# A graph-attention layer: look_rows moved behind the weights, lookups without an addition, low parts in two wide operations, counts cleared on ScalarE

## The chip, the cores and the metric

The kernel runs on one core of a Trainium2 chip. A core has a matrix engine (PE), a vector engine (DVE), a scalar engine (ACT), a general engine that here only issues gathers (POOL), and a queue engine for other transfers (SP). The metric is the device time of one execution in microseconds; the kernel before is given by the median of three executions.

## The reference

There are 12500 nodes with 64 features, 400000 edges with 64 features each, a source node `src` drawn evenly and a target node `dst`; the edges are sorted by target, and low targets have far more edges than high ones. All numbers are float32.

```
e     = leaky_relu(concat(x[src], x[dst], edge) @ W_attn + b_attn, 0.01)[:, 0]
m     = concat(x[src], edge) @ W_ne
alpha = softmax of e over the edges of each target
z     = segment_sum(alpha[:, None] * m, dst)
out   = layernorm(x + relu(concat(x, z) @ W_out))
```

## The kernel before

**Groups, lots, batches.** The edges are cut into 782 groups of 512 (128 partitions by T = 4). 678 of them go the ordinary way, in 44 batches, mostly of 16 groups in four lots of four. For each group and t POOL issues one indirect gather (L310) of 128 rows of a table, which holds a node's share of the score and its features; the rows land in `zx`, of which there are eight buffers, two batches' worth. A lot's scores come from its edge rows `ze` (L344, L346), the gathered column (L351), and the target's share through a one-hot `hot` (L353 to L362). Then a batch goes through one segment softmax (L652 to L714): scans along the 128 columns of a line on DVE, and turns of boundary values between partitions and lines by PE (L556, L559) with copies by ACT (L659, L563). The softmax is a generator with four stops; at each of them `dense_step(n)` puts other work between. After it the weights w are made (L749), and PE multiplies them with `zx` (L763): this frees the buffers of `zx` for POOL's next gathers. The products of the first two lots are issued in the same batch, those of the others during the next one; DVE adds their sums at L780 (`add_up`).

**Dense groups.** The first 104 groups have few target nodes each. Their sources are not gathered. In some 35 batches three of them are done beside the ordinary work:

- *Lookups.* `look_row` loads the low parts of the group's source numbers, spread over all partitions, into `low_of`; `look_turn` makes a one-hot of them on ACT (L400, L401); `look_products` multiplies it with the nodes' shares on PE (L411); `look_scores` picks by the high part on DVE (L436 to L440) and adds to `y_dense` (L442). `look_rows` makes the edges' and targets' shares of all three groups (L421 to L428) and writes their sum to `y_dense` (L430).
- *Sums.* When a round of dense groups has been through its softmax, `dense_counts` counts, for one group, the weights by low and high part of the source: ACT makes one-hots of the high parts (L450, L451), DVE the weighted one-hots of the low parts, `lows` (L453), PE multiplies them (L458), and `dense_sum` adds the result to `counts` (L475). After each chunk `node_products` (L525) multiplies counts with the nodes' features, `node_pick` takes what is wanted (L533, L536) and clears `counts` (L538). `edge_products` and `edge_sum` (L510, L518) do the edge part.

**Order.** The program orders PE, DVE, ACT and SP by hand: every engine works in the order of the program. POOL's gathers are issued a batch ahead and wait only for buffers. Inside a batch: at lot 0 the loads of `ed` and `wrow_d` (`look_loads`) and of the first `low_of`; scores of lot 0, `node_products`, `edge_products`; after the scores of lot 1 `add_up`, the second one-hot, the products of the first lookup, and `dense_counts` of the first group; after the scores of lot 2 `look_rows`; scores of lot 3; the softmax with its steps; the weights and the products of lots 0 and 1; `slots_of`, which prepares the batch after next. In step 0 of the softmax stand `node_pick`, `edge_sum`, the first `look_scores` and `dense_sum`; in step 1 the second `look_scores`; in steps 2 and 3 `dense_counts` of the second and third group. `ed`, `wrow_d` and `low_of` have one buffer each.

Of the kernel before, what the change touches and what calls it, by code (L numbers as in the profile page):

```python
# [9 lines left out]
F32 = mybir.dt.float32  # L10
I32 = mybir.dt.int32
AF = mybir.ActivationFunctionType
OP = mybir.AluOpType
AX = mybir.AxisListType

P = 128
T = 4
# [8 lines left out]
S = 48  # L26
BG = 32
BIG = 6
LOWS = 6
SG = 4  # L30
BS = 16
DO = BS + 1
# [10 lines left out]
ND = 16  # L43
# [11 lines left out]
EngineType = mybir.EngineType  # L55


def sorted_path(ctx, tc, x, dst, idx, edge, w_ne, w_attn, b_attn, w_out, out, flag):
# [6 lines left out]
    nc = tc.nc  # L65
    N, D = x.shape
    E = edge.shape[0]
    NB = (N + P - 1) // P
# [6 lines left out]
    within = "a destination is a node"  # L75

    const = ctx.enter_context(tc.tile_pool(name="const", bufs=1))
# [32 lines left out]
    def nodes_of(g):  # L110
        return next(n for upto, n in NODS if g < upto)
# [4 lines left out]
    def round_of(g):  # L116
        return max(d for d in range(DB) if begins[d] <= g)

    def kept_at(g):
        d = round_of(g)  # L120
        return g - begins[d] + d % 2 * BD
# [3 lines left out]
    DN = DBL * P  # L125
# [47 lines left out]
    low, place = (const.tile([P, T, DG], F32, name=n) for n in ("low", "place"))  # L173
    high, slot_ = (const.tile([P, T, DG], BF16, name=n) for n in ("high", "slot_"))
    y_dense = const.tile([P, T, 2 * BD], F32, name="y_dense")
    kept = const.tile([P, T, 2 * BD], F32, name="kept")
# [4 lines left out]
    acce = const.tile([P, DN + NOD], F32, name="acce")  # L181
    nc.vector.memset(acce, 0.0)
    edge_both = const.tile([P, D], F32, name="edge_both")
    dn = const.tile([1, DG + 1], I32, name="dn")
    rel = const.tile([1, DG], I32, name="rel")
    counts = const.tile([P, NB, ND], F32, name="counts")
# [3 lines left out]
    nc.vector.tensor_reduce(node, ident.rearrange("p (h n) -> p n h", n=ND), axis=AX.X, op=OP.add)  # L190
    meet = const.tile([1, 2], I32, name="meet")
    of_next = const.tile([1, 4], F32, name="of_next")
    scrap_row = const.tile([1, 1], F32, name="scrap_row")

    loop = ExitStack()
# [2 lines left out]
    tiny = loop.enter_context(tc.tile_pool(name="tiny", bufs=2))  # L198
# [28 lines left out]
    pens, sixth, count_ = cut(pps, 2 * P, P, P)  # L227
    sixth, w_dst = sixth[:, 0:NB], sixth[:, 0:D]
# [164 lines left out]
    def big():  # L393
        return work.tile([P, P, T], F32, name="big", bufs=BIG)
# [19 lines left out]
    def look_rows(g0, n, loads):  # L414

        ed, wrow = loads
        many = nodes_of(g0)
        assert many == nodes_of(g0 + n - 1)
        pr = feats.tile([P, SG, T, D], F32, name="pr", bufs=1)
        total = tiny.tile([P, 2, EACH, T], F32, name="total")[:, :, 0:n]  # L420
        nc.vector.tensor_tensor(pr[:, 0:n], ed[:, 0:n], w_edge.unsqueeze(1).to_broadcast([P, n, T, D]), op=OP.mult)  # L421
        nc.vector.tensor_reduce(total[:, 0], pr[:, 0:n], axis=AX.X, op=OP.add)
        at = pr[:, 0].rearrange("p t f -> p (t f)")[:, 0:n * T * many].rearrange("p (g t n) -> p g t n", g=n, n=many)
        nc.vector.tensor_tensor(at, slots[:, 0:many].unsqueeze(1).unsqueeze(1).to_broadcast([P, n, T, many]),
                                slot_[:, :, g0:g0 + n].rearrange("p t g -> p g t").unsqueeze(3).to_broadcast([P, n, T, many]),
                                op=OP.is_equal)
        nc.vector.tensor_tensor(at, at, wrow[:, 0:n].unsqueeze(2).to_broadcast([P, n, T, many]), op=OP.mult)
        nc.vector.tensor_reduce(total[:, 1], at, axis=AX.X, op=OP.add)  # L428
        y0 = kept_at(g0)
        nc.vector.tensor_tensor(y_dense[:, :, y0:y0 + n].rearrange("p t g -> p g t"), total[:, 0], total[:, 1], op=OP.add)  # L430

    def look_scores(g, found):

        pr = feats.tile([P, SG, T, D], F32, name="pr", bufs=1)
        hits = pr.rearrange("p g t f -> p (g t f)")[:, 0:T * NB].rearrange("p (t h) -> p t h", t=T)
        nc.vector.tensor_tensor(hits, count_[:, 0:NB].unsqueeze(1).to_broadcast([P, T, NB]),  # L436
                                high[:, :, g:g + 1].to_broadcast([P, T, NB]), op=OP.is_equal)
        nc.vector.tensor_tensor(hits, hits, found, op=OP.mult)  # L438
        picked = tiny.tile([P, T], F32, name="picked")
        nc.vector.tensor_reduce(picked, hits, axis=AX.X, op=OP.add)  # L440
        y = y_dense[:, :, kept_at(g)]
        nc.vector.tensor_tensor(y, y, picked, op=OP.add)  # L442

    def dense_counts(g):

        highs, lows = [], []
        wide = NB * min(FIT, nodes_of(g))
        for t in range(T):
            hi = big().rearrange("l p t -> l (p t)")[:, 0:wide]
            nc.scalar.activation(hi, places[:, 0:wide], AF.Square, bias=place[:, t, g:g + 1])  # L450
            nc.scalar.activation(hi, hi, AF.Relu, scale=-1.0, bias=1.0)  # L451
            lows.append(work.tile([P, P], F32, name="lows", bufs=LOWS))
            nc.vector.tensor_scalar(lows[t], count_, low[:, t, g:g + 1], kept[:, t, kept_at(g):kept_at(g) + 1],  # L453
                                    op0=OP.is_equal, op1=OP.mult)
            highs.append(hi)
        to = psum.tile([P, SG, P], F32, name="pg", bufs=4).rearrange("p a b -> p (a b)")[:, 0:wide]
        for t in range(T):
            nc.tensor.matmul(to, lows[t], highs[t], start=(t == 0), stop=(t == T - 1))  # L458
        if nodes_of(g) > FIT:
            hi = big().rearrange("l p t -> l (p t)")[:, 0:T * NB].rearrange("l (t h) -> l t h", t=T)  # L460
            for t in range(T):
                nc.scalar.activation(hi[:, t], places[:, wide:wide + NB], AF.Square, bias=place[:, t, g:g + 1])
            nc.scalar.activation(hi, hi, AF.Relu, scale=-1.0, bias=1.0)
            for t in range(T):
                nc.tensor.matmul(sixth, lows[t], hi[:, t], start=(t == 0), stop=(t == T - 1), skip_group_check=True)
        return g, to

    def dense_sum(g, to):
# [23 lines left out]
    def node_of(g):  # L492
        _, vs = nc.values_load_multi_w_load_instructions(
            dn[0:1, g:g + 1], engines=(EngineType.DVE,), min_val=0, max_val=DN - 1,
            skip_runtime_bounds_check_because=within)
        return vs[0]
# [15 lines left out]

    def edge_sum(g0, n, z):

        for c in range(n + n % 2):
            of = slice(c % 2 * D, (c % 2 + 1) * D)
            at = acce[of, ds(node_of(g0 + min(c, n - 1)), nodes_of(g0))]
            nc.vector.tensor_tensor(at, at, z[of, c, :], op=OP.add)  # L518

    def node_products(g0):  # L520
# [8 lines left out]
    def node_pick(g0, pairs):  # L529

        pr = feats.tile([P, SG, T, D], F32, name="pr", bufs=1)
        mine = pr[:, 0:2].rearrange("p g t f -> p (g t) f")
        nc.vector.tensor_tensor(mine, pairs.rearrange("p (h f) -> p h f", f=D),  # L533
                                own.unsqueeze(2).to_broadcast([P, HC, D]), op=OP.mult)
        sums_ = work.tile([P, D], F32, name="sums_", bufs=1)
        nc.vector.tensor_reduce(sums_, mine.rearrange("p h f -> p f h"), axis=AX.X, op=OP.add)  # L536
        if g0 + chunk_sizes[-1] < DG:
            nc.vector.memset(counts, 0.0)  # L538
        return g0, sums_

    def node_turn(g0, sums_, bank_):
# [213 lines left out]
    def bank(k):  # L755
        return psum.tile([P, SG, P], F32, name="pg", bufs=4)[:, :, 0:widths[k]]
# [62 lines left out]
    with before:  # L819
# [22 lines left out]
        with tc.manual_schedule(engines={EngineType.DVE, EngineType.Pool, EngineType.Activation, EngineType.PE, EngineType.SP}):  # L842
# [21 lines left out]
            for g0 in range(0, NG, 3 * P):  # L864
                n = min(3 * P, NG - g0)
# [5 lines left out]
            at = 0  # L871
# [32 lines left out]
    work = loop.enter_context(tc.tile_pool(name="work", bufs=2))  # L904
# [131 lines left out]
    k = 0  # L1036
# [6 lines left out]
    with loop:  # L1043
# [36 lines left out]
        loads = rows_again = None  # L1080
# [18 lines left out]
        with tc.manual_schedule(engines={EngineType.PE, EngineType.DVE, EngineType.Activation, EngineType.SP}):  # L1099
            ready, turns = {}, []  # L1100
            resting, batch_looks, batch_counts = None, [], []
# [9 lines left out]
            for k, G in enumerate(sizes):  # L1111
# [6 lines left out]
                if k:  # L1118
                    joined = resting
                    batch_looks = alike(looks)  # L1120
# [10 lines left out]
                for i, (g0, n) in enumerate(lots[k]):  # L1131
                    if g0 in follows:
                        ahead_of(*follows[g0])
                    if k and i == 0 and batch_looks:
                        loads = look_loads(batch_looks[0], len(batch_looks))
# [23 lines left out]
                        seen.append((batch_looks[0], look_products(turns.pop(0), shared)))  # L1159
                    if k == 1 and i == 1:  # L1160
                        nc.vector.memset(counts, 0.0)
                    if k and i == 2 and batch_looks:
                        look_rows(batch_looks[0], len(batch_looks), loads)
                    if k and i == 1 and batch_counts:
                        open_counts.append(dense_counts(batch_counts[0]))
                    if i == 3 and batch_counts:
# [71 lines left out]
                if fac_d is not None and k > fac_at[1]:  # L1238
                    at = node_of(fac_at[0])
# [42 lines left out]
                for i, (g0, n, zx, hot) in enumerate(parts):  # L1282
                    w = weights(g0, n, hot, b0)
                    if i == 0:
                        while open_counts:
                            dense_sum(*open_counts.pop(0))
                    if i < NOW:
                        pg = bank(k)
                        products(k, pg, zx, w, range(n))
                        sums.append((g0, n, pg, b0, fac if i == 0 else None))  # L1290
                    else:
                        later.append([k, g0, n, zx, w, b0, None, 0, None])
                if more:
                    ready[k + 2] = slots_of(k + 2)
            add_up()
# [442 lines left out]
```

## Time and profile before

| | |
|---|---|
| median of three runs | 4354.64 us (4350.4 to 4369.21) |
| the profiled execution | 4348.44 us, span 4346.6 us |
| granted clock of PE, mean | 0.666 |
| busy share of PE, DVE, ACT, POOL | 53%, 49%, 27%, 59% |
| POOL's gathers, L310 | 2648 of 944 ns |

The columns of a group's row are: line, engine, operation, output and inputs with their shapes, count; then busy time in us and mean ns of one; then the idle time of the engine just before them, and what ended it. A row of a timeline has start and length in us, and in brackets the engine's idle time before it and what ended that. A row of the waits has the total of the waiting in us, how many times, and the longest. "issue" means that nothing was found to wait for, "remote" that the event could not be traced to an instruction.

### The profile page before, as it was taken

The page shows a single profiled execution, that of the slowest core. Times are in us where ns is not written, and L with a number is a line of the kernel's source. Part 1 is how long each engine was busy: PE and PEld are TensorE (multiplying, and loading weights), DVE is VectorE, ACT ScalarE, POOL GpSimd, SP SyncE. Part 2 cuts the span into 40 slices and gives each one's busy share as a digit, 9 for nine tenths or more (in the row PEclk, how much of TensorE's full clock was granted, in tenths as well). Part 3 has the DMA queues.
Part 4 walks back from the last instruction along what each step waited for, and adds up shares of the span by engine and source line. Part 5 has one row for each costly group of instructions (what it writes and reads, how often), then busy time and mean ns, then how long its engine had stood idle before and what let it go on. Part 6 is the DMA issues. An engine that isn't in the chain of part 4 may idle for free. (4 is left out here: it accounts for less than half of the span.)

```text
span 4346.6 us, 35943 instructions
## 1 busy us (share of the span) xinstructions
PE 2307.0 (53%) x9391; PEld 1840.8 (42%) x9391; DVE 2116.4 (49%) x5395; ACT 1165.9 (27%) x2586; POOL 2568.5 (59%) x2728
## 2 busy tenths in 40 slices
PE   0143344554555554655566665666566655565843
PEld 0143344444444444444444443444444434443543
DVE  4343344444444454554445554555555444453645
ACT  0111122222222232222223232332333223333312
POOL 6666666666556666566555655566555645555462
PEclk9999996555555555666566666666666656565655
DMA  9232223223232232322222222222223212222221
GB/s 116 57 64 52 53 55 73 56 56 69 45 67 57 55 63 58 68 54 57 56 58 63 60 55 56 56 57 58 56 57 74 57 31 47 50 49 43 58 46 26
DMA packets 497933, 248.42 MB, mean 57 GB/s; under 512 B 332351, under 2 KB 454286, under 8 KB 497718
## 3 DMA queue, kind: packets, MB, share of 16 engines
q1 hardware_dynamic: 407506, 155.16, 15.2%
q0 software_dynamic: 87008, 90.47, 13.6%
q8 instruction: 78, 1.28, 0.1%
q10 hardware_dynamic: 3204, 0.39, 0.1%
q14 instruction: 137, 1.12, 0.1%
HBM read 239.02 MB, written 6.77 MB: 57 GB/s over the span
## 5 line engine op out<-in xcount | busy, mean ns | idle before, releaser
L310 POOL DMA_INDIRECT zx<-table,srcs x2648 | 2499.3, 944 | 1683.0 <-issue 1239.6
L763 PE MATMUL pg<-w,zx 128*128 128x16 f32 (+9 forms) x5280 | 1042.6, 359 | 602.6 <-issue 548.0
L763 PEld LDWEIGHTS pg<-w,zx 128*128 128x128 f32 x5280 | 1061.4, 302 | 608.1 <-issue 549.0
L458 PE MATMUL pg<-big,lows 128*128 128x490 f32 (+3 forms) x832 | 493.3, 747 | 486.1 <-DVE lows L453 204.2
L458 PEld LDWEIGHTS pg<-big,lows 128*128 128x128 f32 x832 | 237.5, 300 | 669.7 <-issue 473.5
L525 PE MATMUL pg<-xall,counts 128*128 128x512 f32 (+1 forms) x650 | 326.7, 664 | 4.4 <-DVE var L1024 2.4
L344 DVE TENSOR_TENSOR pr<-ze,fixed 128x1024 f32<-128x1024 f32 (+3 forms) x176 | 207.5, 1179 | 224.4 <-issue 95.5
L411 PE MATMUL pg<-s_src,big 128*128 128x98 f32 x832 | 228.2, 433 | 164.1 <-issue 145.0
L556 PE MATMUL lines<-ident,bnd 128*1 128x128 f32 x176 | 52.8, 391 | 462.7 <-issue 342.1
L450 ACT ACTIVATE big<-places,place 128x490 f32<-128x490 int16 (+3 forms) x416 | 249.5, 600 | 155.3 <-remote 153.2
L411 PEld LDWEIGHTS pg<-s_src,big 128*128 128x128 f32 x832 | 209.0, 327 | 171.2 <-issue 170.6
L475 DVE TENSOR_TENSOR counts<-counts,pg 128x490 f32 (+3 forms) x104 | 58.1, 558 | 391.4 <-remote 311.4
L780 DVE TENSOR_TENSOR acc<-acc,pg 128x32 f32 (+9 forms) x678 | 125.8, 186 | 234.2 <-PE pg L763 106.0
L438 DVE TENSOR_TENSOR pr<-pr,pg 128x392 f32<-128x392 f32 x104 | 58.5, 562 | 354.9 <-remote 175.3
L346 DVE TENSOR_REDUCE fixed<-pr 128x16 f32<-128x1024 f32 (+3 forms) x176 | 209.2, 1188 | 32.2 <-issue 14.0
L451 ACT ACTIVATE big<-big 128x490 f32<-128x490 f32 (+3 forms) x416 | 217.2, 522 | 13.2
L556 PEld LDWEIGHTS lines<-ident,bnd 128*1 128x1 f32 x176 | 14.6, 98 | 485.9 <-issue 360.1
L525 PEld LDWEIGHTS pg<-xall,counts 128*128 128x128 f32 (+1 forms) x650 | 137.6, 219 | 188.8 <-issue 188.8
L563 ACT ACTIVATE line<-tops 1x256 f32<-1x256 f32 x44 | 29.0, 659 | 624.7 <-DVE tops L665 381.6
L342 ACT ACTIVATE zx<-ze 128x1024 f32<-128x1024 f32 (+3 forms) x176 | 181.0, 1028 | 8.3 <-issue 1.3
L341 ACT ACTIVATE fixed<-wrow 128x144 f32<-128x144 f32 (+9 forms) x176 | 46.0, 262 | 506.7 <-issue 321.7
L453 DVE TENSOR_SCALAR lows<-pps,low,kept 128x128 f32<-128x128 f32 x416 | 141.5, 403 | 0.0
(335 smaller groups left out, 2474.2 us busy)
## 6 DMA issues: line engine op xcount, KB each, us to landing
ze<-in_edge_dram SPq DMA_DIRECT2D x160, 512.0 KB
zx<-table,srcs POOLq DMA_INDIRECT x2648
low_of<-low_rows SPq DMA_DIRECT2D x104, 128.0 KB
ep<-in_edge_dram SPq DMA_DIRECT2D x104, 128.0 KB
ed<-in_edge_dram SPq DMA_DIRECT2D x34, 384.0 KB
table<-xall SPq DMA_DIRECT2D x7, 455.0 KB
ze<-in_edge_dram SPq DMA_DIRECT2D x8, 384.0 KB
out_dram<-yo SPq DMA_DIRECT2D x23, 128.0 KB
```

The lines of the kernel that those rows point to most:

```text
L310: nc.gpsimd.indirect_dma_start(out=zx[0:r, g, t, 1:EW] if plain else zx[0:r, g, t, 0:EW], out_offset=None, in_=x[:, :] if plain else table ...
L342: nc.scalar.activation(zx[0:r, 0:n, :, EW:EW + D], ze[0:r, 0:n], AF.Copy)
L344: nc.vector.tensor_tensor(pr[0:r, 0:n], ze[0:r, 0:n], w_edge[0:r].unsqueeze(1).to_broadcast([r, n, T, D]), op=OP.mult)
L346: nc.vector.tensor_reduce(ysum[0:r, 0:n], pr[0:r, 0:n], axis=AX.X, op=OP.add)
L411: nc.tensor.matmul(found[:, t, :], hot[:, :, t], s_src, start=True, stop=True)
L450: nc.scalar.activation(hi, places[:, 0:wide], AF.Square, bias=place[:, t, g:g + 1])
L451: nc.scalar.activation(hi, hi, AF.Relu, scale=-1.0, bias=1.0)
L453: nc.vector.tensor_scalar(lows[t], count_, low[:, t, g:g + 1], kept[:, t, kept_at(g):kept_at(g) + 1], op0=OP.is_equal, op1=OP.mult)
L458: nc.tensor.matmul(to, lows[t], highs[t], start=(t == 0), stop=(t == T - 1))
L525: nc.tensor.matmul(pairs[0:m * ND, 0:m * D], counts[:, h0:h0 + m, :].rearrange("l h n -> l (h n)"), xall[:, h0:h0 + m, 1:EW], start=(h0 == ...
L763: nc.tensor.matmul(pg[:, g, :], zx[:, g, t, 1:EW + D], w[:, g, t, :], start=(t == 0), stop=(t == T - 1))
L780: nc.vector.tensor_tensor(ag, ag, pg[:, g, :], op=OP.add)
```

## The change

Four edits:

1. `look_rows` is called after the batch's weights, ahead of `slots_of`, in place of after the scores of lot 2. `look_scores` now comes first and writes `y_dense` by its reduction; `look_rows` adds its total to it, by one addition more.
2. `dense_counts` makes the low parts of a group by two operations of 128x512 (compare, multiply) in place of four fused ones of 128x128, ahead of ACT's one-hots; three buffers of 128x4x128 in place of six of 128x128.
3. `edge_sum` loads its register values in one call instead of one for each column.
4. `counts` is cleared by an activation on ACT that copies a zero column, in place of a memset on DVE.

```diff
-LOWS = 6
+LOWS = 3
...
+    zero_col = const.tile([P, 1], F32, name="zero_col")
+    nc.vector.memset(zero_col, 0.0)
...
     # look_rows
         nc.vector.tensor_reduce(total[:, 1], at, axis=AX.X, op=OP.add)
         y0 = kept_at(g0)
-        nc.vector.tensor_tensor(y_dense[:, :, y0:y0 + n].rearrange("p t g -> p g t"), total[:, 0], total[:, 1], op=OP.add)
+        nc.vector.tensor_tensor(total[:, 0], total[:, 0], total[:, 1], op=OP.add)
+        y = y_dense[:, :, y0:y0 + n].rearrange("p t g -> p g t")
+        nc.vector.tensor_tensor(y, y, total[:, 0], op=OP.add)
...
     # look_scores
         nc.vector.tensor_tensor(hits, hits, found, op=OP.mult)
-        picked = tiny.tile([P, T], F32, name="picked")
-        nc.vector.tensor_reduce(picked, hits, axis=AX.X, op=OP.add)
-        y = y_dense[:, :, kept_at(g)]
-        nc.vector.tensor_tensor(y, y, picked, op=OP.add)
+        nc.vector.tensor_reduce(y_dense[:, :, kept_at(g)], hits, axis=AX.X, op=OP.add)
...
     # dense_counts
-        highs, lows = [], []
+        highs = []
+        lows = work.tile([P, T, P], F32, name="lows", bufs=LOWS)
+        nc.vector.tensor_tensor(lows, count_.unsqueeze(1).to_broadcast([P, T, P]),
+                                low[:, :, g:g + 1].to_broadcast([P, T, P]), op=OP.is_equal)
+        nc.vector.tensor_tensor(lows, lows, kept[:, :, kept_at(g):kept_at(g) + 1].to_broadcast([P, T, P]), op=OP.mult)
...
-            lows.append(work.tile([P, P], F32, name="lows", bufs=LOWS))
-            nc.vector.tensor_scalar(lows[t], count_, low[:, t, g:g + 1], kept[:, t, kept_at(g):kept_at(g) + 1],
-                                    op0=OP.is_equal, op1=OP.mult)
...
-            nc.tensor.matmul(to, lows[t], highs[t], start=(t == 0), stop=(t == T - 1))
+            nc.tensor.matmul(to, lows[:, t], highs[t], start=(t == 0), stop=(t == T - 1))
...
     # edge_sum
+        _, vs = nc.values_load_multi_w_load_instructions(
+            dn[0:1, g0:g0 + n], engines=(EngineType.DVE,), min_val=0, max_val=DN - 1,
+            skip_runtime_bounds_check_because=within)
...
-            at = acce[of, ds(node_of(g0 + min(c, n - 1)), nodes_of(g0))]
+            at = acce[of, ds(vs[min(c, n - 1)], nodes_of(g0))]
...
     # node_pick
-            nc.vector.memset(counts, 0.0)
+            nc.scalar.activation(counts.rearrange("p h n -> p (h n)"), zero_col.to_broadcast([P, NB * ND]), AF.Copy)
...
     # the loop over batches
-                    if k and i == 2 and batch_looks:
-                        look_rows(batch_looks[0], len(batch_looks), loads)
...
+                if batch_looks:
+                    look_rows(batch_looks[0], len(batch_looks), loads)
                 if more:
                     ready[k + 2] = slots_of(k + 2)
```

More of the change, by code (lines that the diff above doesn't have):

```diff
@@ L464, in dense_counts @@
             for t in range(T):
-                nc.tensor.matmul(sixth, lows[t], hi[:, t], start=(t == 0), stop=(t == T - 1), skip_group_check=True)
+                nc.tensor.matmul(sixth, lows[:, t], hi[:, t], start=(t == 0), stop=(t == T - 1), skip_group_check=True)
         return g, to
```

## The prediction

> **What bounds the kernel now.** I read the page first (engine shares, costliest groups), then the waits of all engines, then the timeline of each engine through several batches of the middle of the span.
>
> ```profile
> span 4346.6 us, 35943 instructions
> PE 2307.0 (53%) x9391; PEld 1840.8 (42%) x9391; DVE 2116.4 (49%) x5395; ACT 1165.9 (27%) x2586; POOL 2568.5 (59%) x2728
> L310 POOL DMA_INDIRECT zx<-table,srcs x2648 | 2499.3, 944 | 1683.0 <-issue 1239.6
> ```
>
> No engine is full. POOL is the busiest, and its row tells more than its share: 2648 gathers of 944 ns each. These rows of PE's and POOL's timelines show how the gathers follow each other, and two places where they don't:
>
> ```profile
> 1857.70 0.58 PE L556 MATMUL lines<-ident,bnd 128*1 128x128 f32 x2 [10.79 <-ACT bnd L659]
> 1858.08 4.30 PE L763 MATMUL pg<-w,zx 128*128 128x28 f32 x20
> ...
> 1835.64 0.94 POOL L310 DMA_INDIRECT zx<-table,srcs  x1 [4.14 <-ACT nfar L597]
> ...
> 1874.35 0.94 POOL L310 DMA_INDIRECT zx<-table,srcs  x1 [0.30 <-issue]
> 1882.37 0.94 POOL L310 DMA_INDIRECT zx<-table,srcs  x1 [7.08 <-issue]
> ```
>
> With nothing to hold it POOL leaves 0.30 us between two gathers. A full batch has 64 of them, so POOL alone needs 64 × 1.25 = 80 us for a batch. What it loses beyond that it loses at a few places, where a gather waits for a buffer of zx that PE's weighted products (L763) of two batches earlier still read: 4.14 us at one, 7.08 us at the other. (What the profile names as releaser there is only what ended last; a gather waits for none of ACT's tiles.) Ahead of the longer one PE stood idle for 10.79 us until the boundaries of the batch's segments (bnd) came from DVE by way of ACT; only then could it go on with the products that free buffers. What DVE did meanwhile:
>
> ```profile
> 1838.99 0.84 DVE L780 TENSOR_TENSOR acc<-acc,pg 128x28 f32 x4 [3.21 <-PE pg L763]
> 1839.74 1.36 DVE L453 TENSOR_SCALAR lows<-pps,low,kept 128x128 f32<-128x128 f32 x4
> 1841.02 0.28 DVE L599 CUSTOM_DVE_ANT_0 step<-far 128x129 f32<-128x129 f32 x1
> ...
> 1842.88 1.22 DVE L344 TENSOR_TENSOR pr<-ze,fixed 128x1024 f32<-128x1024 f32 x1 [1.57 <-ACT pen L604]
> ...
> 1847.58 0.18 DVE L362 TENSOR_TENSOR soft<-fixed,sdst 128x16 f32<-128x16 f32 x1
> 1847.67 0.94 DVE L421 TENSOR_TENSOR pr<-ed,fixed 128x768 f32<-128x768 f32 x1
> 1848.65 0.95 DVE L422 TENSOR_REDUCE total<-pr 128x12 f32<-128x768 f32 x1
> 1849.64 0.21 DVE L424 TENSOR_TENSOR pr<-fixed,slot__119 128x48 f32<-128x48 f32 x1
> 1849.88 0.21 DVE L427 TENSOR_TENSOR pr<-pr,wrow_d 128x48 f32<-128x48 f32 x1
> 1850.12 0.20 DVE L428 TENSOR_REDUCE total<-pr 128x12 f32<-128x48 f32 x1
> 1850.36 0.18 DVE L430 TENSOR_TENSOR y_dense<-total 128x12 f32<-128x12 f32 x1
> 1850.45 1.22 DVE L344 TENSOR_TENSOR pr<-ze,fixed 128x1024 f32<-128x1024 f32 x1
> ...
> 1857.01 0.43 DVE L657 TENSOR_TENSOR_SCAN soft<-step,soft 128x128 f32<-128x128 f32 x1
> ```
>
> From 1842.88 on, DVE works without a gap, and PE's idle time ends when DVE is through. The six operations of look_rows (L421 to L430) take 1847.67 to 1850.45, 2.8 us, in the middle of that path. That is one kind of batch. I went through PE's first boundary turn of each of the 35 batches with look_rows; in 17 of them PE had been idle for 10 us or more, from
>
> ```profile
> 229.73 0.58 PE L556 MATMUL lines<-ident,bnd 128*1 128x128 f32 x2 [22.66 <-issue]
> ...
> 3649.51 0.59 PE L556 MATMUL lines<-ident,bnd 128*1 128x128 f32 x2 [15.75 <-ACT bnd L659]
> ```
>
> as the first and the last of the 17. In the other 18 PE has no idle time there, or 2 us, since it is itself behind with earlier products; what DVE gains in these is hidden. All sums below are of changes and are set against the profiled run, 4348.4 us (span 4346.6); the median of the runs, 4354.6, is 0.14% above it, and I add the change to the median.
>
> **A. look_rows moved to the end of the batch.** It leaves DVE's path in 17 batches: 17 × 2.8 = 48 us at most. How much of it POOL gives back depends on its stall after it: 7.08 us above, where the shorter kind of stall has 4.14, so I take 7.08 − 4.14 = 2.9 us as what can be had, all of the 2.8, where the stall is like this one. I count 60%, −28 us, since the next batch is of the other kind as often as not and can take the gain back as PE's lateness. In a few batches look_rows lies in a stretch in which all engines go slowly, one operation per 1.40 us:
>
> ```profile
> 2052.02 0.21 DVE L424 TENSOR_TENSOR pr<-fixed,slot__119 128x48 f32<-128x48 f32 x1 [0.44 <-DVE total L422]
> 2053.42 0.21 DVE L427 TENSOR_TENSOR pr<-pr,wrow_d 128x48 f32<-128x48 f32 x1 [1.20 <-DVE pr L424]
> 2054.82 0.20 DVE L428 TENSOR_REDUCE total<-pr 128x12 f32<-128x48 f32 x1 [1.19 <-issue]
> ```
>
> There the six take about 7 us instead of 2.8, which PE's lateness mostly covers; I add −4 us over the kernel. Bounds of A: 0 (all hidden) to −62 us (the 17 at full price and 14 from slow stretches).
>
> At its new place look_rows delays DVE's next scores by 2.8 + 0.2 us (one more addition of a few elements, as L430). Cover: DVE's wait for PE in the next batch, 3.21 us at 1838.99. Without that cover it costs what it saves. More delicate is what reads behind it. The tiles ed, wrow_d and low_of have one buffer each; SP loads the next batch's ed and wrow_d only when look_rows has read them, and low_of (which ACT's L400 needs) is queued on SP behind those, and behind low_of the edge rows (ze) of a later lot. The rows of ACT and SP:
>
> ```profile
> 1821.12 0.27 ACT L341 ACTIVATE fixed<-wrow 128x112 f32<-128x112 f32 x1 [3.98 <-DVE w L749]
> ...
> 1822.41 0.70 ACT L400 ACTIVATE big<-low_of,p_col 128x512 f32<-128x512 bf16 x1
> ...
> 1826.51 0.27 ACT L341 ACTIVATE fixed<-wrow 128x112 f32<-128x112 f32 x1 [2.21 <-DVE pr L358]
> ...
> 1834.90 0.19 ACT L597 ACTIVATE nfar<-edges_of 128x1 f32<-128x1 int32 x1
> SPq L390 <- DMA low_of<-low_rows: 115.2, 40, 5.9
> ```
>
> The weights end at 1821.1, look_rows would end at 1824, low_of would be issued at about 1825 and land 115.2/40 = 2.9 us later. So L400 moves from 1822.4 to about 1827.8, and behind it on ACT wait the copies of the next lot, the highs of dense_counts and L597, on which DVE's L599 at 1841.02 depends. From L400 to the end of L597 were 12.7 us, 2.2 of them idle before L341 and covered now; with about 2 us of wait for the second low_of it ends near 1840.3. That is inside 1841.02 by some 0.7 us: I cost it at nothing, and it is the thinnest cover of the change (a rival below). The later ze is needed two lots on, at DVE's L344 of 1842.88 at the earliest, and has the same cover.
>
> **B. Low parts by two operations of 512.** The four of 128 take 1.36 us as a group (above, at 1839.74). The nearest row for 512 elements with two tensor inputs:
>
> ```profile
> L533 DVE TENSOR_TENSOR pr<-pg,own 128x512 f32<-128x512 f32 x25 | 17.2, 689 | 193.8 <-remote 167.7 <-PE pg L458 23.6 <-PE pg L411 2.5
> L453 DVE TENSOR_SCALAR lows<-pps,low,kept 128x128 f32<-128x128 f32 x416 | 141.5, 403 | 0.0
> PE pg L458 <- DVE lows L453: 204.2, 27, 32.3
> PE pg L458 <- DVE acc L780: 72.3, 21, 9.1
> ```
>
> Two by 0.69 is 1.38 us: DVE itself gains and loses nothing. But before, PE could begin its first product when the first low part was there, 0.40 us after the start; now none is there before 1.38 us. Where PE stands waiting, its start moves by 0.98 us. The waits name 27 + 21 = 48 groups of 104 where PE's idle time ended with the lows or with the DVE operation just ahead of them: 48 × 0.98 = 47 us at most. By the code the second and third group of a batch stand in the last two steps of the softmax; the second's lateness falls ahead of a POOL stall of the 4-us kind that comes anyway, so I leave it out (24 × 0.98 = 24 us stay), and of the third's I take somewhat over half: +14 us. Bounds 0 and +47 (+68 were all 69 second and third groups on the path).
>
> One rule speaks against B's second operation. It multiplies two SBUF tiles, where the old form read one operand from PSUM. By the Trainium skill (SBUF — State Buffer, "Who interferes with whom") a VectorE instruction with two SBUF inputs contends with a GpSimd instruction that reads SBUF, and one of them blocks. L344 has two such inputs too, and beside the one of 1842.88 to 1844.10 the trace has
>
> ```profile
> 1843.13 0.94 POOL L310 DMA_INDIRECT zx<-table,srcs  x1 [0.30 <-issue]
> ```
>
> a gather of the usual length. I take nothing for it; were every gather beside such an operation held for its 0.69 us, it would be 104 × 0.69 = 72 us.
>
> **C. The small removals.**
>
> ```profile
> L442 DVE TENSOR_TENSOR y_dense<-y_dense,picked 128x4 f32<-128x4 f32 x104 | 17.6, 169 | 9.4 <-DVE picked L440 5.4 <-issue 0.6
> L538 DVE MEMSET counts<- 128x1568 f32 x24 | 32.8, 1365 | 6.6 <-issue 6.6
> L342 ACT ACTIVATE zx<-ze 128x1024 f32<-128x1024 f32 x160 | 169.6, 1060 | 7.7 <-issue 1.3 <-DMA zx<-table,srcs 0.4
> ACT line L563 <- DVE tops L665: 381.6, 26, 29.5
> ```
>
> The additions of the lookups: 17.6 + 9.4 = 27 us of DVE. They stand in the steps between the softmax's yields, where DVE mostly waits for PE; I take a fifth, −5. The clears: 32.8 + 6.6 = 39 us of DVE go to ACT, where one costs about 1060 × 1568/1024 = 1.6 us by L342. ACT stands there with nothing to do until DVE's L665 (26 waits, 14.7 us each), so ACT pays nothing. On DVE the clear and the register loads of edge_sum come while PE is still behind with its first lookups; I take −1. Bounds of C: 0 to −25.
>
> **The sum:** −28 − 4 + 14 − 5 − 1 = −24 us; 4354.6 − 24 = 4330.6, so **4330 us** (0.56% less; the profiled run would be 4324). What a measurement of this kernel can tell from no change is about 0.5%, 22 us.
>
> **The rivals.**
>
> *Hidden anyway.* POOL's 80 us per batch and the stalls that come in all batches set the time, and PE's lateness of 18 batches passes to the other 17. For: half of the batches show no idle PE. Against: the idle times of 10 to 32 us ahead of L556. Then B's and A's terms are both small: 4345 to 4360.
>
> *The whole gain.* A at full price, B hidden: −62 to −70, 4290.
>
> *Slower: low_of comes too late.* Its place is L400, then L597 and L599, ahead of the 17 paths. If ed's load, ahead of it in the queue, makes it land 4 us later than I count, L599 is 4 − 0.7 = 3.3 us late; 17 × 3.3 = 56 us, and with −24 that is +32, 4387. It decides from the 0.7 us on. For: the longest of SP's 40 waits for such a load is 5.9 us. Against: their mean is 2.9.
>
> *Slower or level: the low parts as a block.* All 48 places on the path, +47, or all 69, +68, with −38 for A and C: 4364 to 4385.
>
> *Gathers held by the two-input operation:* +72 − 24, 4402.
>
> **How the numbers follow.** Forecast (4305 to 4348) 0.45, of which 0.30 is faster by over 0.5%; the whole gain 0.10; hidden 0.14; block of low parts 0.11, half of it within 0.5%; low_of late 0.18; gathers held 0.02. So faster 0.40, same 0.15 + 0.14 + 0.05 = 0.34, slower 0.06 + 0.18 + 0.02 = 0.26. The range reaches from the whole gain to low_of late, 4288 to 4398, and leaves out about 0.15; the forecast's own is 4305 to 4348.
>
> **What would show it.** Right: in the profile after, PE's idle time before L556 is shorter by 2 to 3 us in some 17 batches, POOL's stalls of 6 to 9 us fall to 4 to 6, and DVE goes from L362 of the third lot straight to L344 of the fourth. B: two operations of about 0.69 us at the new line, PE's waits for lows longer by 1 us each. C: ACT's clear of 1.5 us ahead of an idle stretch. Wrong: L400 with waits for low_of longer than 6 us and L599 later than PE's L763; gathers longer than 0.95 us beside the multiplication; or POOL's stalls as long as before at places that I did not look at.

## The result and the profile after

The changed kernel takes 4374.54 us (median of 20 runs, 4359.01 to 4384.31), the kernel before 4356.37 (20 runs beside them): a ratio of 1.0036, 95% interval 1.0021 to 1.0050. That is 18 us slower, where 24 us faster was forecast. It lies inside the range of 4288 to 4398, but on the other side of zero. The profiled execution took 4367.78 us. Its page, the rows that answer to those shown of before (L312 was L310, L460 was L458, L561 was L556):

```profile
span 4366.1 us, 35202 instructions
PE 2310.6 (53%) x9391; PEld 1838.7 (42%) x9391; DVE 2077.9 (48%) x5095; ACT 1204.8 (28%) x2610; POOL 2579.0 (59%) x2728
L312 POOL DMA_INDIRECT zx<-table,srcs x2648 | 2509.7, 948 | 1697.2 <-issue 1181.5
L460 PE MATMUL pg<-big,lows 128*128 128x490 f32 (+3 forms) x832 | 507.0, 766 | 580.6 <-DVE lows L451 333.0
L561 PE MATMUL lines<-ident,bnd 128*1 128x128 f32 x176 | 52.2, 389 | 355.9 <-issue 225.2
```

The groups of the three lines before, with the same columns:

```profile
L458 PE MATMUL pg<-big,lows 128*128 128x490 f32 (+3 forms) x832 | 493.3, 747 | 486.1 <-DVE lows L453 204.2
L556 PE MATMUL lines<-ident,bnd 128*1 128x128 f32 x176 | 52.8, 391 | 462.7 <-issue 342.1
```

DVE is busy for 38 us less. PE stands 107 us less ahead of the boundary turns (462.7 to 355.9): look_rows did leave the path. But it stands 94 us more ahead of the products of dense_counts (486.1 to 580.6), and POOL, which paces the batches, has gained nothing: its idle time went from 1683.0 to 1697.2 us, and its gathers now take 2509.7 us in place of 2499.3, 948 ns each in place of 944. The last two differences, 14 and 10 us, are somewhat more than the 19.5 us by which the span grew (4346.6 to 4366.1). The 10 us are 38 gathers of over 1.0 us, where before had 5; the 14 us compare two single traces, and the runs of the kernel before lie up to 45 us apart.

The new operations, by shape, and the waits of ACT and DVE that the moved look_rows could have lengthened:

```profile
L451 DVE TENSOR_TENSOR lows<-lows,kept 128x512 f32<-128x512 f32 x104 | 72.5, 697 | 3.6
L543 ACT ACTIVATE counts<-zero_col 128x1568 f32<-128x1568 f32 x24 | 36.2, 1507 | 336.7 <-PE lines L561 147.7 <-remote 112.5 <-PE pg L460 49.4
L434 DVE TENSOR_TENSOR y_dense<-y_dense,total 128x12 f32<-128x12 f32 x34 | 6.2, 181 | 1.2
ACT big L402 <- DMA low_of<-low_rows: 64.7, 25, 5.0
DVE step L604 <- ACT far L600: 73.7, 5, 35.9
```

The sizes are those of the prediction (0.69 us, 1.5 us against an estimate of 1.6, 0.18 us). ACT now waits 25 times for low_of, 2.6 us in the mean; DVE's wait for L600 has hardly moved (69.0 us in 4 before). So low_of comes later, as foreseen, and its cover held.

### The profile page after: what moved, and what is told of

Same layout as the page of the kernel before. It is cut to its first block, busy times and chain, and to the rows that moved or that the text cites. A ratio compares the mean times of both kernels' runs of the same rounds, so it can differ in the third digit from the quotient of the medians.

```text
span 4366.1 us, 35202 instructions
## 1 busy us (share of the span) xinstructions
PE 2310.6 (53%) x9391; PEld 1838.7 (42%) x9391; DVE 2077.9 (48%) x5095; ACT 1204.8 (28%) x2610; POOL 2579.0 (59%) x2728
## 3 DMA queue, kind: packets, MB, share of 16 engines
q8 instruction: 76, 1.25, 0.1%
## 5 line engine op out<-in xcount | busy, mean ns | idle before, releaser
L312 POOL DMA_INDIRECT zx<-table,srcs x2648 | 2509.7, 948 | 1697.2 <-issue 1181.5
L460 PE MATMUL pg<-big,lows 128*128 128x490 f32 (+3 forms) x832 | 507.0, 766 | 580.6 <-DVE lows L451 333.0
L460 PEld LDWEIGHTS pg<-big,lows 128*128 128x128 f32 x832 | 244.7, 308 | 779.8 <-issue 630.6
L530 PE MATMUL pg<-xall,counts 128*128 128x512 f32 (+1 forms) x650 | 325.7, 662 | 10.9 <-DVE var L1029 5.9
L561 PE MATMUL lines<-ident,bnd 128*1 128x128 f32 x176 | 52.2, 389 | 355.9 <-issue 225.2
L538 DVE TENSOR_TENSOR pr<-pg,own 128x512 f32<-128x512 f32 x25 | 17.2, 688 | 348.4 <-PE lines L561 148.9
L344 ACT ACTIVATE zx<-ze 128x1024 f32<-128x1024 f32 (+3 forms) x176 | 180.7, 1026 | 6.4 <-issue 1.1
L561 PEld LDWEIGHTS lines<-ident,bnd 128*1 128x1 f32 x176 | 14.1, 96 | 387.6 <-issue 266.2
```

Source lines behind the costliest of these rows:

```text
L312: nc.gpsimd.indirect_dma_start(out=zx[0:r, g, t, 1:EW] if plain else zx[0:r, g, t, 0:EW], out_offset=None, in_=x[:, :] if plain else table ...
L344: nc.scalar.activation(zx[0:r, 0:n, :, EW:EW + D], ze[0:r, 0:n], AF.Copy)
L460: nc.tensor.matmul(to, lows[:, t], highs[t], start=(t == 0), stop=(t == T - 1))
L530: nc.tensor.matmul(pairs[0:m * ND, 0:m * D], counts[:, h0:h0 + m, :].rearrange("l h n -> l (h n)"), xall[:, h0:h0 + m, 1:EW], start=(h0 == ...
L561: nc.tensor.transpose(in_order(line), col, ident)
```

## The experiments

The kernels of one study ran on one chip beside the kernel before; the fourth study took two chips. The chips were of two kinds: on some the kernel before takes 4324 to 4356 us, on others 3462 to 3465, so ratios are compared and not times. I call the first the stalling chips, since POOL stops there in every batch, and the others the steady ones. Each chip of the studies was used for one set of runs, so whether this belongs to the chip or to the hour is not known. The only trace of the kernel before is of a stalling chip, the one of the result.

### First: which edit costs (a stalling chip, before at 4343.3 us)

`lows_alone` has the edit of dense_counts alone, `no_lows` the other three alone, `rows_alone` look_rows and look_scores alone. `lows_psum` is the changed kernel with a multiply that reads the counter row in PSUM in place of the comparison's result (its sums are then of other numbers):

```diff
-        nc.vector.tensor_tensor(lows, lows, kept[...], op=OP.mult)
+        nc.vector.tensor_tensor(lows, count_.unsqueeze(1).to_broadcast([P, T, P]), kept[...], op=OP.mult)
```

> The kernel before with the low parts alone by two operations of 512; the other three edits are not made. Theory G (the multiply, which has two SBUF inputs, lengthens gathers that it meets): gathers' busy time up by about 10 us from 2499, some 30 gathers over 1.1 us, and the time up by about 10 us (4366). Theory W (PE waits for the whole block of low parts): gathers as before, PE's waits for the lows up from 204 us, POOL's stalls up, time up by 10 to 20 us. Theory R (look_rows at its new place, or the clear on ACT, costs it all): time as before within 5 us.

> The changed kernel with the low parts undone (four operations of 128 again). G and W: the 18 us go away and what A and C of the prediction promise comes out, time 4356 or less, down to 4330 if A was right. R: time stays at 4370 to 4375.

> The changed kernel, but the second operation on the low parts reads the counter row in PSUM instead of the first one's result, so one of its inputs is no longer in SBUF; its length and place stay. The low parts then hold products of the counter and the weight, so the sums over sources are of other numbers. G: the long gathers go away (2499 us again instead of 2510) and the time falls by about 10 us against the changed kernel, to 4364. W and R: time as the changed kernel, 4374, within 4 us.

> The kernel before with look_rows alone moved behind the weights, and the lookups without an addition. Prediction's A: 4356 - 28 to - 37 = 4320 to 4328. Rival (the gain of the path is taken back in the softmax, since PE and POOL come no earlier): within 6 us of before. Rival (low_of too late): 4370 or more, with L599 waiting for ACT.

Measured, as ratio to before: lows_alone 1.0031 (1.0013 to 1.0050), no_lows 1.0009 (0.9993 to 1.0025), lows_psum 1.0038 (1.0022 to 1.0055), rows_alone 1.0003 (0.9985 to 1.0020). The wide operations alone cost as much as the whole change; look_rows and the small removals bring nothing that can be told, where A and C had promised 0.9%. Theory R falls. So does theory G as the whole cost on this chip: without the two SBUF inputs the long gathers are gone (2 of over 1.0 us, where after has 38), and the time did not come down. The trace of lows_alone says the same: its gathers take 5 us more than those of before (2504.7 against 2499.3), of some 14 us measured.

Why the look_rows that left the path brings nothing is seen in the batch that the prediction showed. PE and POOL of rows_alone (L555, L762 and L310 there), timeline:

```profile
1832.40 0.94 POOL L310 DMA_INDIRECT zx<-table,srcs  x1 [4.17 <-ACT big L400]
...
1852.22 0.59 PE L555 MATMUL lines<-ident,bnd 128*1 128x128 f32 x2 [7.40 <-issue]
1852.60 2.82 PE L762 MATMUL pg<-w,zx 128*128 128x28 f32 x13
1856.04 0.20 PE L762 MATMUL pg<-w,zx 128*128 128x28 f32 x1 [0.63 <-issue]
1858.84 0.20 PE L762 MATMUL pg<-w,zx 128*128 128x28 f32 x1 [2.60 <-issue]
...
1874.94 0.20 PE L762 MATMUL pg<-w,zx 128*128 128x28 f32 x1 [2.59 <-issue]
1877.04 0.20 PE L762 MATMUL pg<-w,zx 128*128 128x28 f32 x1 [1.90 <-issue]
1877.76 2.32 PE L762 MATMUL pg<-w,zx 128*128 128x28 f32 x10 [0.52 <-issue]
...
1880.83 0.94 POOL L310 DMA_INDIRECT zx<-table,srcs  x1 [8.79 <-issue]
```

and the same of before, past the rows shown in the prediction:

```profile
1858.08 4.73 PE L763 MATMUL pg<-w,zx 128*128 128x28 f32 x22
1865.40 0.20 PE L763 MATMUL pg<-w,zx 128*128 128x28 f32 x1 [2.59 <-issue]
1868.19 0.20 PE L763 MATMUL pg<-w,zx 128*128 128x28 f32 x1 [2.59 <-issue]
...
1880.82 0.81 PE L763 MATMUL pg<-w,zx 128*128 128x28 f32 x3 [0.52 <-issue]
```

The boundary came 5.5 us earlier (1852.22 against 1857.70); 3.2 us of this POOL had already before the batch (1832.40 against 1835.64), so 2.2 us are the batch's own. PE's idle time there fell from 10.79 to 7.40 us. But then PE does 13 products quickly instead of 22, and after that one in 2.8 us, until it is quick again at 1877.76, some 6 us after POOL has run out of buffers (1880.83 − 8.79 = 1872.04); before, it is quick again at 1880.82, 5.5 us after POOL had stopped at 1875.29. The slow products begin 24 us after POOL's resumption at 1832.40, and 27 us after the one of 1835.64 before. In this batch, what PE gains ahead of the slow stretch it loses in it: in both traces the stretch ends some 6 us after POOL has stopped, not by when PE began. POOL's stall even grew, from 7.08 to 8.79 us. That is one batch; for the whole kernel POOL's row of rows_alone shows that the stalls did not shrink (1683.0 us idle before),

```profile
L310 POOL DMA_INDIRECT zx<-table,srcs x2648 | 2499.5, 944 | 1680.1 <-issue 1219.8
L555 PE MATMUL lines<-ident,bnd 128*1 128x128 f32 x176 | 52.0, 388 | 367.3 <-issue 196.2
```

while PE's idle time ahead of the boundary turns fell by 95 us (462.7 to 367.3).

### Second: lateness, the last batches, and another form (a steady chip, before at 3463.8 us)

In the traces of after and lows_alone one batch stood out. PE's timeline of lows_alone:

```profile
3884.29 0.29 PE L560 MATMUL lines<-ident,line 1*128 1x1 f32 x2
...
3919.71 6.53 PE L459 MATMUL pg<-big,lows 128*128 128x490 f32 x8 [35.14 <-DVE lows L450]
```

and PE's and POOL's of before:

```profile
3881.99 0.28 PE L559 MATMUL lines<-ident,line 1*128 1x1 f32 x2
...
3892.61 0.94 POOL L310 DMA_INDIRECT zx<-table,srcs  x1 [3.77 <-issue]
...
3894.79 5.97 PE L458 MATMUL pg<-big,lows 128*128 128x490 f32 x8 [12.51 <-DVE lows L453]
```

Before, POOL paused for 3.77 us and DVE and PE went on; in lows_alone POOL did not pause there, and PE stood for 35 us. Most of the loss of these two traces arises here: of the 2648 gathers, the 2421st starts 0.8 us earlier in lows_alone than in before and the 2433rd 15.8 us later; in after the lag goes from 6.5 to 21.5 us. From that I formed theory T: all of the cost lies in this batch. `rev` issues the four operations in the order t = 3, 2, 1, 0; `two_late` and `two_early` choose by the group:

```diff
+        if g >= 96:          # two_early: g < 96
             (two operations of 512)
+        else:
+            for t in range(T):
+                nc.vector.tensor_scalar(lows[:, t], count_, low[:, t, g:g + 1], kept[...], op0=OP.is_equal, op1=OP.mult)
```

and `fold` leaves only the comparison on DVE and lets ACT bring the weights in:

```diff
-            nc.scalar.activation(hi, hi, AF.Relu, scale=-1.0, bias=1.0)
+            nc.scalar.activation(hi, hi, AF.Relu, scale=nkept[:, t, c:c + 1], bias=kept[:, t, c:c + 1])
```

> The kernel before; the four operations on the low parts are issued in the order t = 3, 2, 1, 0, while PE still takes t = 0 first. So PE can start only after the last of them (1.36 us, as the two wide ones) and nothing else is changed. If lateness for PE (W) is what the wide operations cost: the same +0.3% as they had alone, 4355 to 4360 where before is 4343. If it is something else of theirs (the gathers, the instructions' number): as before, within 5 us.

> The kernel before with the two wide operations for groups 96 to 103 alone (the last batches that count) and four of 128, into one tile, for the others. Theory T (all of the cost falls in the one batch after 3850 us, where POOL goes past its 48th gather without a pause and PE, DVE and ACT stand till the next): time as with the wide operations everywhere, +12 to +18 us. Theory W spread over all batches: +1 us (8 of 104).

> The complement: two wide operations for groups 0 to 95, four of 128 for the last eight. T: as before, within 5 us. W, spread over all batches: +12 to +14 us.

> The kernel before with one operation of 512 on the low parts (the comparison alone); the weights come in on ACT, as scale and offset of its second operation on the high parts. Low parts are there after 0.69 us instead of 0.40 (first of four) or 1.38 (two), DVE works 0.67 us less per group, 104 x 0.67 = 70 us less busy; no operation has two SBUF inputs. W: +0.29/0.98 of the wide ones' cost, +4 us, less what DVE's time brings, so -10 to +5. T: it depends on whether the pause of the batch after 3850 us is kept; without it +12 to +18.

Measured: rev 0.9999 (0.9990 to 1.0008), two_late 1.0002 (0.9992 to 1.0011), two_early 1.0033 (1.0021 to 1.0045), fold 1.0001 (0.9992 to 1.0010). two_early costs 10.9 us (3474.67 against 3463.77). The gathers of rev, two_late and two_early, in this order, from their pages:

```profile
L310 POOL DMA_INDIRECT zx<-table,srcs x2648 | 2502.3, 945 | 806.9 <-issue 740.7
```
```profile
L310 POOL DMA_INDIRECT zx<-table,srcs x2648 | 2500.6, 944 | 807.1 <-issue 741.3
```
```profile
L310 POOL DMA_INDIRECT zx<-table,srcs x2648 | 2512.6, 949 | 806.9 <-issue 742.6
```

All three have the same idle time, 807 us, most of it the 0.30 us between two gathers: on this chip POOL never stops and sets the time. So rev and fold, level here, say nothing of lateness on a stalling chip, and two_late and two_early say nothing of theory T. What it takes longer shows in full: 2512.6 − 2502.3 = 10.3 us against 10.9 measured. And this is where it comes from, two places of the timeline of two_early:

```profile
464.22 0.68 DVE L449 TENSOR_TENSOR lows<-pps,low 128x512 f32<-128x512 f32 x1
464.39 0.94 POOL L310 DMA_INDIRECT zx<-table,srcs  x1 [0.30 <-issue]
...
1727.60 0.94 POOL L310 DMA_INDIRECT zx<-table,srcs  x1 [0.30 <-issue]
1727.97 0.68 DVE L449 TENSOR_TENSOR lows<-pps,low 128x512 f32<-128x512 f32 x1
1728.69 0.69 DVE L451 TENSOR_TENSOR lows<-lows,kept 128x512 f32<-128x512 f32 x1
1728.85 1.35 POOL L310 DMA_INDIRECT zx<-table,srcs  x1 [0.30 <-issue]
...
1730.50 0.94 POOL L310 DMA_INDIRECT zx<-table,srcs  x1 [0.30 <-issue]
```

The gather that starts 0.16 us into the multiply takes 0.41 us longer; the one that starts 0.17 us into a comparison L449, which reads one operand in PSUM (pps), does not. So it is throughout the trace: of the 51 gathers that start under an L451, 34 take over 1.0 us, the longest 1.47; of the 60 that start under an L449 none does; and of the 69 that had begun before an L451 none does, so only some of the 96 multiplies hold one. By the Trainium skill (SBUF — State Buffer, "Who interferes with whom") a VectorE instruction with two SBUF inputs contends with a GpSimd instruction that reads SBUF; this trace agrees, with 1.35 us in place of 0.94.

### Third: the same on a stalling chip (before at 4323.5 us)

> The changed kernel once more, for a second profile. Where the kernel before takes about 3464 us (POOL never stops there, 2712 gathers by 1.25 us and what lies around them): theory G gives + 10 us, gathers' busy time up by 10 us. Where it takes about 4350 us: +0.36% as before, and a second trace tells whether the batch after 3850 us loses its pause again (theory T).

> The changed kernel with the counter row in PSUM as the first input of the second operation (the sums are then of other numbers). Where before takes 3464 us: G says as before, within 2 us, with no long gathers. Where it takes 4350 us: +0.38% as it had, if G is a small part there.

> The kernel before with the four operations on the low parts in the order t = 3, 2, 1, 0, PE taking t = 0 first. Where before takes 4350 us: W (lateness for PE is the cost) +0.3%; otherwise as before. Where before takes 3464 us: as before, since POOL sets the time.

> The kernel before with the two wide operations for groups 96 to 103 alone. Where before takes 4350 us: T (the cost falls in the batch after 3850 us) +12 to +18 us; W spread over all batches +1 us. Where before takes 3464 us: as before, +1 us at most from gathers.

Measured: after_again 1.0030 (1.0014 to 1.0047), lows_psum_again 1.0021 (1.0010 to 1.0032), rev_again 1.0008 (0.9993 to 1.0023), two_late_again 0.9982 (0.9969 to 0.9996). The loss repeats. T falls: the wide operations in the last groups alone cost nothing, and the trace of rev_again, without them, has a batch after 3817 us that is as long as that of after_again (118 and 117 us from one transpose at the softmax's start to the next, where before took 94). That pause is lost or kept for another reason. As before was not traced on this chip, it is not known whether it keeps the pause here; rev_again loses it and is level with before all the same. Why two_late_again is 0.18% faster was not found either; the wide tile alone (wide4, below) was not run on a stalling chip. Against lows_psum_again the gathers may be a part of the loss, 0.1%, which the intervals do not tell from nothing; lateness alone, in rev_again, is at most 0.23%, and the wide operations without long gathers, together with the other three edits, are at least 0.10%.

### Fourth: the controls (steady chips, before at 3461.6 and 3464.6 us)

`wide4` has four operations of 128 into the wide tile, `wide4_rev` the same in reverse order, `psum_alone` the two wide operations with PSUM as the multiply's first input and none of the other edits (its sums, too, are of other numbers); fold once more. wide4_rev and psum_alone were run again on a second chip.

> The kernel before, with its four operations writing parts of one tile of 128x4x128 (three buffers) as in the changed kernel. It is the control of the two after it: the tile and its buffers alone. Theory W and theory G: as before or a few us less (three groups of low parts fit in place of one and a half), -6 to 0 us.

> As wide4, with the four in the order t = 3, 2, 1, 0, so that PE's first product waits for the last: lateness alone. W: where before takes 4320 to 4350 us, +6 to +14 us against wide4; where it takes 3464 us, nothing. If lateness is not the cost: within 4 us of wide4 on both.

> The kernel before with the two wide operations, the second one reading the counter row in PSUM instead of the first one's result (one SBUF input; the sums are of other numbers). W: as wide4_rev within 4 us, since PE waits as long. G: where before takes 3464 us, as before (two wide operations with two SBUF inputs took 11 us more there). If it is slower than wide4_rev by 5 us or more, something else of the wide operations costs.

> The kernel before with the comparison alone on DVE (0.69 us) and the weights as scale and offset of ACT's second operation. Where before takes 3464 us: as before, as it was. Where it takes 4320 to 4350 us: W gives 0.29/0.98 of wide4_rev's cost, 2 to 4 us, less what 70 us less of DVE's time bring: -10 to +4 us.

> Four operations into the wide tile in the order t = 3, 2, 1, 0; PE waits for the last. Where before takes 4320 to 4350 us: W says +0.2 to +0.3% (all of the wide operations' cost there); if lateness is not the cost, -0.2 to +0.1%. Where it takes 3464 us, as before.

> Two wide operations without the two SBUF inputs, none of the other edits. Where before takes 4320 to 4350 us: W says the same as wide4_rev_again within 0.1%. If it is slower than that by 0.2% or more, neither lateness nor the gathers are the cost, but something of the wide operations themselves. If it is as before, the gathers were the cost there too. Where it takes 3464 us, as before.

Measured: wide4 1.0000 (0.9991 to 1.0009), wide4_rev 1.0000 (0.9991 to 1.0009), psum_alone 0.9999 (0.9990 to 1.0008), fold_again 0.9999 (0.9990 to 1.0008); wide4_rev_again 0.9998 (0.9989 to 1.0007), psum_alone_again 0.9995 (0.9986 to 1.0004). Both chips were steady ones, so the question that these runs were made for, lateness on a stalling chip, stays open. What they do show is the other half of the second study: psum_alone's gathers are

```profile
L310 POOL DMA_INDIRECT zx<-table,srcs x2648 | 2499.3, 944 | 807.1 <-issue 741.9
```

13 us less than two_early's, with two operations of the same length (0.68 and 0.69 us), and the time is that of before within 0.1%. (Some 3 of the 13 us are the chip: rev has 2502.3 beside two_early.) On a steady chip the cost of the wide operations is the second SBUF input, to within that 0.1%.

## Why the prediction was wrong

**A failed, and with it the sign.** The step "60% of what can be had, −28 us, and −4 us from slow stretches" measured +0.03% (−0.15% to +0.20%), between −7 and +9 us. That look_rows leaves the path was right, and about by its 2.8 us: in the batch shown the boundary came 2.2 us earlier, counted from POOL's resumption, and PE's idle time there was 3.4 us shorter. What failed is the next step, that POOL's stall would shrink with it, from 7.08 towards 4.14 us: it grew to 8.79 us there, and over the kernel POOL's idle time is 1680.1 us in rows_alone against 1683.0. In the batch shown a slow stretch takes the gain, such as the prediction showed with its rows at 1.40 us a step and used as an extra gain: PE's products come one in 2.1 to 2.8 us until some 6 us after POOL has stopped. The rival "hidden anyway" (0.14) was the right one for A, though, in the batch shown, by this mechanism and not by the lateness of 18 batches.

**B: size right, reason not shown.** +14 us was forecast, lows_alone measured +0.31% (0.13% to 0.50%), some 14 us. The reason given was PE's wait for the whole block; rev_again, which has that and nothing else, is at +0.08% (−0.07% to +0.23%). PE's waits for the lows did grow (204.2 us in 27 to 333.0 us in 38), but rev_again has as many,

```profile
PE pg L459 <- DVE lows L455: 330.1, 44, 33.6
```

and is level with before. As far as the runs show, that the size came out was luck.

**The two-input operation was put aside on a wrong reading.** The prediction held L344's usual gather against the rule, "L344 has two such inputs too". It has not: the row names its second input `fixed`, and that is a tile in PSUM,

```
fixed = psum.tile([P, 512], F32, name="fixed", bufs=1)
slots, w_edge, alpha, win, ysum, scrap = cut(fixed, S, D, T * BG, SG * S, SG * T, 8)
```

so L344 reads one input from SBUF and was no counterexample. Of the 153 gathers that start under an L344 in before, none takes over 0.96 us. With a chance of 0.02 and 72 us this rival was wrong in both: it is real, shown on steady chips, and costs 10 to 11 us there, since only some of the multiplies meet the start of a gather, and those hold it for 0.3 us in the mean (10.8 us over 34).

**C** was −6 us; together with A it is +0.09% (−0.07% to +0.25%) in no_lows. DVE is busy for 41 us less there (2075.0 against 2116.4), and no gain from it can be told. The way of low_of was sized by the wrong row, the mean of SP's own waits, 2.9 us, and not the time from issue to landing; but its cover held, and rows_alone, which has the later low_of, is at +0.03%, so the rival priced at 4387 us did not come; the block of low parts (0.11) gave times near the measured one, but its mechanism is not what was shown.

**What stays open** is what the wide operations cost on stalling chips beyond the gathers: without the second SBUF input they still took 0.38% (0.22% to 0.55%) and 0.21% (0.10% to 0.32%) with the other edits in. Lateness for PE, the other edits (0.09%) and where POOL's pauses fall can each be part of it; no run separates them. In the traces of after and lows_alone some 15 us of the loss come with the one pause that POOL misses, and what decides that pause was not found. No version was shown to beat both kernels: fold, which takes 70 us from DVE and has no two-input operation, is level with before on steady chips and was not run on a stalling one; two_late was 0.18% faster there and level on a steady one.

## What to carry to other kernels

Before a row is used as a counterexample, look up in the code in which memory each of its operands lives; a name in the profile does not say it. A step taken off one engine's path is a gain only if the stall of the engine that paces the work shrinks with it, and that is asked of the stall, not of the path. Where gathers run back to back on POOL, as on the steady chips here, let a wide DVE operation beside them read one input from PSUM (psum_alone, 0.9999), or give the multiplication to ACT as a scale (fold, 1.0001).

## What the runs showed of the hardware

The same program took 4324 to 4356 us on some chips and 3462 to 3465 on others, 25% apart. On the steady ones the slow stretches are gone: PE's idle time ahead of the weighted products is 7.3 us in all in rev, where the same kernel has 643.5 on a stalling chip (rev_again),

```profile
L764 PE MATMUL pg<-w,zx 128*128 128x16 f32 (+9 forms) x5280 | 1040.7, 369 | 7.3 <-DVE w L750 7.0
L764 PE MATMUL pg<-w,zx 128*128 128x16 f32 (+9 forms) x5280 | 1039.6, 357 | 643.5 <-issue 592.8
```

with a granted clock of 0.694 against 0.663, 5% apart where the times are 25% apart. On the steady chips a batch takes 80 us, just the 64 gathers by 1.25 us. What holds PE, DVE and ACT on the stalling chips while POOL gathers without a pause was not found.
